# Another table of places for the attention stage's jobs

## The chip, the cores and the metric

The kernel runs on one core of one Trainium2 chip. The metric is the device time of one execution in microseconds (us), as the median of a few runs. TensorE (PE) multiplies matrices, VectorE (DVE) and ScalarE (ACT) read its results from PSUM, GpSimd (POOL) works on SBUF alone, SyncE (SP) issues most transfers. PEld is TensorE's loading of weights, which overlaps its products.

## The reference

Four graph layers work one after the other on 16 graphs of 1024 nodes with 128 features. Only the first of them is touched. It scores pairs of nodes and takes a softmax over the neighbours:

```python
h_self = node_features @ W_self_w + W_self_b
h_nb = node_features @ W_nb_w + W_nb_b
pre = (h_self @ A1_i)[:, :, None, :] + (h_nb @ A1_j)[:, None, :, :] + A1_b
scores = (relu(pre) @ A2_w)[..., 0] + A2_b[0]
scores = where(adjacency == 0, -1e9, scores)
agg = einsum('bij,bjf->bif', softmax(scores), h_nb)
x = layernorm(x + relu(h_self + agg))
```

The adjacency has few edges (a probability of about 0.8% for a pair, and it is symmetric), so the kernel finds the edges and works on them alone. The layers behind (a dilated graph convolution, a dense one and a normalised one) stay as they are.

## The kernel before

`phase_att` does the first layer. The nodes of a graph are cut into NG = 10 groups of W = 104 nodes. A pair of groups (i, j) with j >= i is a *unit*, and a graph has 55. They stand in 5 *blocks* of UNITS = 11: block r holds the pairs of groups r and 9 - r. So there are 16 x 5 = 80 blocks and 880 units. A graph is also called a batch here, and r runs from 0 to 4 within it.

Time is counted in *slots*, one for each unit. Each unit has a gather, a score, a weigh and a scatter. The gather (L554, L559) brings both ends' features for up to 128 edges to a bank `pg`. The score is VectorE's, L571, once for each direction. ScalarE's weigh is an exponential (L581) and a scaled copy (L583) to `hg`. The scatter (L592) adds `hg` into the sums `pa`, with the selection matrix `we`; scatters come some three units behind their gather (BEHIND), and pause at the head of a batch for the units in PAUSE, until the batch before has been collected (L603) and its banks cleared (L300).

The rest of a block's work prepares blocks ahead. Each kind has up to three parts, for units 0 to 3, 4 to 7 and 8 to 10:

- `count` (L401), `offset` (L412) and `rank` (L436, L442) number the edges of a unit; ScalarE copies the results (L408, L417, L449).
- GpSimd's `beyond` (L423) subtracts the offsets from a row of numbers into the tile `g`, of which there is one buffer. VectorE clamps it to 0..1 (`clamp`, L431).
- `step` (L464) turns `g` into selection matrices for an edge's first end; ScalarE copies them (L473) into `oh_b`. `other` (L480) finds the second end; VectorE's comparison (L488) reads it. `widen` (L494) copies both for the gathers.
- `number` (L500, read at L507) and `numbered` (L539, on VectorE) make `we` for the scatters.
- `one_way` (L456) checks on VectorE that the adjacency is symmetric.

For the next batch there are two projections a block (L343, L346; read by ScalarE in L353, L357, L360 and by VectorE in L364 `low` and L367 `add_z`; L371 is `self_score`), and masks: a load of rows, GpSimd's comparison (L316, L318) and a store. For the batch before there is the end: `end_group` (L636, L639 and the statistics L78, L79 on VectorE), a root on GpSimd (`end_root`), `end_norm` (L657 on ScalarE), and transposes (L673, read at L677).

Step, other, rank and its companions, projections and transposes all put their products in the pool `ps_w`, which has **two** PSUM banks. They take turns: a job can start only when all readers of the job two before it are done.

The order is written out. Each job has a place, a number in slots counted from its block's or its batch's first slot:

```python
for key, parts in BANKS:
    ...
        do(at, key, lambda parts: bank_products([(kind, k, block(y)) for kind, k, y in parts]), parts)
        for kind, k, y in parts:
            do(at, READ[kind, k], lambda *key: held.pop(key)(), kind, k, y)
```

All jobs are sorted by place and issued in that order. Each engine keeps its own instructions in it (`as_traced`). A gather stands at u + 0.2, a score at u + 0.55, a scatter at u + 0.8. A place below 0 or above 11 lies in the block before or behind, so that -2.05 is 8.95 of the block before. The places say nothing on time as such: an engine that is done goes on to its next instruction, and one that lacks something holds up all behind it.

Of the kernel before, what the change touches and what calls it, by code (L numbers as in the profile page):

```python
# [130 lines left out]
def as_traced(tc, first):  # L131
# [10 lines left out]


BANKS = (
    (-2.05, (("step", 0),)), (-0.7, (("step", 1),)), (1.5, (("step", 2),)), (2.05, (("other", 0),)),
    (3.1, (("other", 1),)), (4.42, (("rank", 1),)), (5.5, (("rank", 0), ("count", 0),)), (5.58, (("other", 2),)),
    (6.38, (("rank", 2), ("number", 0), ("offset", 0),)),
)
READ = {
    ("step", 0): -1.5, ("step", 1): 0.05, ("step", 2): 1.85, ("rank", 0): 5.82, ("count", 0): 5.75, ("other", 0): 2.5,  # L150
    ("other", 1): 4.36, ("other", 2): 5.9, ("rank", 1): 4.9, ("rank", 2): 7.05, ("offset", 0): 8.31,
    ("number", 0): 7.56,
}
PROJECT = (
    (6.25, 6.42, 6.54, 7.25, 7.33, 6.85, 16.48), (9.85, 9.9, 10.6, 9.95, 11.38, 11.56, 17.53),
)
BEYOND = (3.72, 5.65, 6.42)
CLAMP = (6.38, 8.56, 11.15)
NUMBERED = (1.38, 5.32, 9.9)
ONE_WAY = (-2.25, 5.95)  # L160
WIDEN = (3.38, 6.02, 8.53)
SCORE, WEIGH, SCATTER = 0.55, 1.01, 0.8
COLLECT = (3.51, 3.52, 5.3)
CLEAR = (7.38, 5.9, 6.25)
DIVIDE = 6.45
END_GROUP = (6.58, 9.33, 16.31, 13.9, 28.75, 29.9, 20.38, 27.32, 17.78, 25.5)
END_ROOT = 30.1
END_NORM = (36.72, 38.51, 33.95, 34.54, 38.53, 33.78, 36.32, 43.54, 42.75, 42.53)
END_STORE = 45.1
TURN = ((46.25, 46.65), (47.38, 49.31), (51.45, 51.85))  # L170
MASKS = (-85.1, -82.25, -66.44, -55.48, -52.46, -49.25, -45.47, -42.18, -35.52, -29.18)
AHEAD = {"step": 1, "other": 1, "number": 1, "rank": 2, "count": 3, "offset": 3}
PAUSE = (3, 4, 5, 6)
BEHIND = 3


# [1 line left out]
def phase_att(ctx, tc, t, c, x1_d, x1T_d, mask_d, keep, flags):  # L178
# [207 lines left out]
    def pieces():  # L386
        return [(n0, min(4, UNITS - n0)) for n0 in range(0, UNITS, 4)]

    def block(x):

        if x not in V and x < B * BANDS:
            v = V[x] = Consts()
            v.x = x
            b, v.r = divmod(x, BANDS)
            v.d, v.mt, v.q, v.todo = S[b], MT[b % 2], QS[x % 2], band(v.r)
        return V.get(x)
# [22 lines left out]
    def beyond(v, n0, m):  # L419

        if n0 == 0:
            v.g = sm.tile([P, UNITS, C], F16, name="g", bufs=1)
        nc.gpsimd.tensor_tensor(  # L423
            v.g[:E, n0 : n0 + m, :], k_next[:E].unsqueeze(1).to_broadcast([E, m, C]),
            v.off[:, n0 : n0 + m].unsqueeze(2).to_broadcast([E, m, C]), ALU.subtract,
        )

    def clamp(v, n0, m):

        g = v.g[:E, n0 : n0 + m, :]  # L430
        nc.vector.tensor_scalar(g, g, 1.0, 0.0, op0=ALU.min, op1=ALU.max)  # L431
# [19 lines left out]
    def one_way(v, half):  # L451

        i = (v.r, NG - 1 - v.r)[half]
        at, nb = half * (NG - v.r), NG - i
        junk = sm.tile([P, NG, W], BF16, name="one_way", bufs=1)
        nc.vector.scalar_tensor_tensor(  # L456
            junk[:W, :nb, :], v.q[:W, at : at + nb, :W], EDGE,
            v.mt[:W, i, i * W : NP].rearrange("p (n w) -> p n w", w=W),
            op0=ALU.is_ge, op1=ALU.not_equal, accum_out=seen_one_way[:W, v.x, half : half + 1],
        )  # L460
# [32 lines left out]
    def widen(v, n0, m):  # L493
        nc.scalar.copy(v.ends[:W, n0 : n0 + m], v.o[:W, n0 : n0 + m])  # L494
# [207 lines left out]
    def do(slot, key, f, *args):  # L702
        todo.append((slot + key, len(todo), f, args))

    def scatters(b, n):
        owed.append((b, *divmod(n, UNITS)))
        if not (b and n in PAUSE):
            for _ in range(2 if len(owed) > BEHIND + 1 else 1):
# [34 lines left out]
    for x in range(-3, B * BANDS):  # L743
# [7 lines left out]
        for k in range(3 if x >= 0 else 0):  # L751
            do(at, NUMBERED[k], numbered, b, r, *CHUNKS[k])
        for key, parts in BANKS:
# [5 lines left out]
        for k in range(3):  # L759
            if 0 <= x + 2 < B * BANDS:  # L760
                do(at, BEYOND[k], lambda y, k: beyond(block(y), *pieces()[k]), x + 2, k)
                do(at, CLAMP[k], lambda y, k: clamp(block(y), *pieces()[k]), x + 2, k)
            if 0 <= x + 1 < B * BANDS:
                do(at, WIDEN[k], lambda y, k: widen(block(y), *pieces()[k]), x + 1, k)
        for k in range(2):
            if 0 <= x + 1 < B * BANDS:
                do(at, ONE_WAY[k], lambda y, k: one_way(block(y), k), x + 1, k)
            if 0 <= x and b + 1 < B:
# [4 lines left out]
    for b in range(B - 1):  # L773
# [4 lines left out]
        for s in range(NG):  # L778
            key = MASKS[s] if b else 2 * s - SLOTS + 0.05
            do(at, key - 3 if b else max(key - 3, -SLOTS), load_rows, b + 1, s)  # L780
# [3 lines left out]
        for k in range(3):  # L784
            do(at, COLLECT[k], collect, b, k)
            do(at, CLEAR[k], clear, k)
            do(at, TURN[k][0], open_turn, b, k)
            do(at, TURN[k][1], close_turn, b, k)
        do(at, DIVIDE, end_seen, b)
        do(at, DIVIDE, end_divide, b)  # L790
        do(at, DIVIDE, lambda b: nc.gpsimd.memset(OWN[b % 2][:W, :, 0, F : F + 1], 1.0), b)
        for s in range(NG):
            do(at, END_GROUP[s], end_group, b, ORDER[s])
            do(at, END_NORM[s], end_norm, b, s)
        do(at, END_ROOT, end_root, b)
# [1768 lines left out]
```

## Time and profile before

| | |
|---|---|
| median of 3 runs | 2990.48 us (2989.75 to 2993.03) |
| the profiled execution's own time | 2983.48 us |
| span of its instructions | 2981.2 us |
| mean granted TensorE clock | 0.951 |
| attention stage | to about 1565 us |
| TensorE, VectorE, ScalarE, GpSimd busy, 420 to 720 us | 286.40, 257.49, 251.53, 158.55 us |

A group in the profile has a line of the kernel, an engine, an operation, its tiles (out<-in), shapes, a count, the busy time in us with the mean in ns, and behind the second bar the engine's idle time just before these instructions with what ended it. A timeline row has the start, the duration, the engine, the line and, in brackets, the idle time before it.

### The profile page before, as it was taken

What the parts mean: (1) busy time and instruction counts of PE and PEld (TensorE: products, weight loads), DVE (VectorE), ACT (ScalarE), POOL (GpSimd) and SP (SyncE); (2) the same over time, 40 slices, a digit from 0 to 9 for tenths busy, and PEclk for the clock granted to TensorE, in tenths of its full rate; (3) what the DMA queues carried; (4) which work ended last, traced back from release to release, by engine and by line L of the source; (5) the groups of instructions that cost most, each with busy time, mean ns of one, the idle gap of its engine ahead of it and who ended that gap; (6) DMA issues with size and microseconds to landing.
All of it is one profiled execution on the core that took longest, in us unless ns stands there. A gap on an engine that the chain in (4) does not pass through costs nothing. (4 is left out here: it accounts for less than half of the span.)

```text
span 2981.2 us, 71230 instructions
## 1 busy us (share of the span) xinstructions
PE 2695.8 (90%) x25811; PEld 2407.9 (81%) x25811; DVE 2246.4 (75%) x8654; ACT 1845.1 (62%) x5689; POOL 1261.2 (42%) x1305
## 2 busy tenths in 40 slices
PE   5999999999999999999997888668897999999997
PEld 3888888888888888888897887457786999999996
DVE  5798888988888888988884467756655667777674
ACT  3887888888887888888873233246753433443333
POOL 3655555644555555654223323244433233333321
PEclk8999999999999999999997777789998999999999
DMA  5324332333224332333215442044555254444540
GB/s 160 91 79 114 87 89 68 101 103 84 82 75 115 87 92 73 93 107 88 61 51 168 167 133 79 21 153 170 181 194 212 100 186 177 151 144 181 186 156 17
DMA packets 179962, 348.64 MB, mean 117 GB/s; under 512 B 14148, under 2 KB 89942, under 8 KB 179472
## 3 DMA queue, kind: packets, MB, share of 16 engines
q1 hardware_dynamic: 173584, 328.15, 34.3%
q0 software_dynamic: 4864, 11.63, 1.3%
q10 hardware_dynamic: 1152, 4.19, 0.5%
q8 instruction: 207, 3.39, 0.5%
q14 instruction: 155, 1.27, 0.1%
HBM read 257.87 MB, written 87.03 MB: 116 GB/s over the span
## 5 line engine op out<-in xcount | busy, mean ns | idle before, releaser
L583 ACT ACTIVATE hg<-pg,hg 128x128 f32<-128x128 f32 x1600 | 511.3, 365 | 28.7
L554 PE MATMUL pg<-parts,oh 104*128 104x384 f32 (+1 forms) x1760 | 521.0, 377 | 0.9 <-ACT hg L583 0.8
L316 POOL TENSOR_SCALAR arena<-ld 104x1024 f16<-104x1024 f32 (+1 forms) x150 | 421.7, 2812 | 234.1 <-DMA ld<-in_adjT 234.1
L592 PE MATMUL pa<-hg,we 128*104 128x129 f32 (+1 forms) x3520 | 517.7, 271 | 0.4 <-DVE we L539 0.4
L592 PEld LDWEIGHTS pa<-hg,we 128*104 128x104 f32 x3520 | 465.4, 171 | 10.2 <-DVE we L539 0.8
L571 DVE SCALAR_TENSOR_TENSOR junk<-pg,w_a 128x128 bf16<-128x128 f32 x1600 | 398.4, 283 | 96.9 <-PE pg L559 94.9
L559 PE MATMUL pg<-parts,oh 104*128 104x384 f32 (+1 forms) x1760 | 438.4, 330 | 0.0
L423 POOL TENSOR_TENSOR g<-k_next,off 105x512 f16<-105x512 f16 (+1 forms) x240 | 241.9, 1027 | 315.4 <-PE pw L464 291.7
L559 PEld LDWEIGHTS pg<-parts,oh 104*128 104x128 f32 x1760 | 313.9, 190 | 0.1
L554 PEld LDWEIGHTS pg<-parts,oh 104*128 104x128 f32 x1760 | 276.5, 192 | 27.6 <-issue 15.1
L1667 POOL TENSOR_TENSOR rstd<-ve,mhalf 128x4 f32<-128x4 f32 x96 | 98.1, 1022 | 440.4 <-DVE ve L1666 440.4
L581 ACT ACTIVATE hg<-sc 128x2 f32<-128x2 f32 (+1 forms) x880 | 189.9, 216 | 151.4 <-DVE junk L571 146.7
L1705 ACT COPY xT<-pt 128x512 f32<-128x512 f32 x64 | 37.5, 586 | 374.9 <-PE pt L1704 343.0
L539 DVE TENSOR_TENSOR we<-k_id,ids 128x832 f32<-128x832 f16 (+1 forms) x240 | 254.4, 1060 | 0.0
L494 ACT CAST oh<-oh_b 104x1024 fp32r<-104x1024 bf16 (+1 forms) x240 | 235.2, 980 | 2.4 <-DVE oh_b L488 2.4
L343 PE MATMUL pw<-w_all,xT 128*104 128x512 f32 x320 | 170.2, 613 | 14.2 <-DMA xT<-in_xTp 9.3
L488 DVE TENSOR_TENSOR oh_b<-pw,k_slot_edge 104x512 bf16<-104x512 f32 (+1 forms) x240 | 153.8, 641 | 15.8 <-PE pw L480 15.4
L364 DVE TENSOR_TENSOR parts<-pw,parts 104x384 fp32r<-104x384 f32 x160 | 88.3, 552 | 86.5 <-ACT own L360 85.6
L473 ACT CAST oh_b<-pw 104x512 bf16<-104x512 f32 (+1 forms) x240 | 131.1, 547 | 0.7 <-PE pw L464 0.3
L571 DVE DVE_READ_ACCUMULATOR junk<-pg,w_a 128x1 f32 x1600 | 131.0, 82 | 0.0
L456 DVE SCALAR_TENSOR_TENSOR one_way<-qs,arena 104x1040 bf16<-104x1040 f16 (+9 forms) x160 | 125.7, 786 | 2.2 <-ACT qs L449 2.2
L1508 DVE BATCH_NORM_STATS2 stats<-pt 128x6 f32<-128x512 f32 x120 | 79.0, 691 | 62.6 <-PE pt L1504 61.4
(368 smaller groups left out, 6477.3 us busy)
## 6 DMA issues: line engine op xcount, KB each, us to landing
ld<-in_adjT SPq DMA_DIRECT2D x135, 416.0 KB
keep_adj<-in_adjT SPq DMA_DIRECT2D x8, 4096.0 KB
adj<-in_adjT SPq DMA_DIRECT2D x8, 4096.0 KB
mask_d<-arena SPq DMA_DIRECT2D x144, 208.0 KB
hT_d<-uT SPq DMA_DIRECT2D x48, 512.0 KB
h<-hT_d SPq DMA_DIRECT2D x48, 512.0 KB
arena<-mask_d SPq DMA_DIRECT2D x11, 2048.0 KB
hT<-hT_d SPq DMA_DIRECT2D x32, 512.0 KB
```

Of the source, the lines that this page charges most:

```text
L316: engine.tensor_scalar(mt[:n, s, :N], ld[:n], 0.0, None, op0=ALU.is_gt)
L343: nc.tensor.matmul(pw[:W], d.xT[:, s * W : (s + 1) * W], w_all, start=True, stop=False, skip_group_check=True)
L423: nc.gpsimd.tensor_tensor(v.g[:E, n0 : n0 + m, :], k_next[:E].unsqueeze(1).to_broadcast([E, m, C]), v.off[:, n0 : n0 + m].unsqueeze(2).to_ ...
L488: nc.vector.tensor_tensor(v.o[:W, n0 : n0 + m, 1, :], pw[:W, : m * C].rearrange("p (n c) -> p n c", c=C), k_slot_edge[:W].unsqueeze(1).to_ ...
L494: nc.scalar.copy(v.ends[:W, n0 : n0 + m], v.o[:W, n0 : n0 + m])
L539: nc.vector.tensor_tensor(we[:, :n, :], k_id.unsqueeze(1).to_broadcast([P, n, W]), V[b * BANDS + r].ids[:, 2 * lo : 2 * hi].unsqueeze(2).t ...
L554: nc.tensor.matmul(flat[:, first : 3 * F], own, d.parts[i][:W, p, first:], start=p == 0, stop=False, skip_group_check=True,)
L559: nc.tensor.matmul(pg[:, 1::step, :], other, reversed_parts(d.parts[j][:W, p, :], step), start=False, stop=p == 1, skip_group_check=True,)
L571: nc.vector.scalar_tensor_tensor(junk, pg[:, 1 + e, :], 0.0, w_a2, op0=ALU.max, op1=ALU.mult, accum_out=d.sc[:, at + e : at + e + 1],)
L581: nc.scalar.activation(hg[:, :ways, F], d.sc[:, at : at + ways], AF.Exp)
L583: nc.scalar.activation(hg[:, e, :F], pg[:, 3 - 3 * e, :], AF.Copy, scale=hg[:, e, F : F + 1])
L592: nc.tensor.matmul(PA[bank][:W, at : at + part.stop - part.start], we[:, 2 * (u - lo) + e, :], hg[:, e, part], start=False, stop=True, ski ...
```

## The change

Only the table of places is changed. The functions, the instructions and the sizes stay.

```diff
 BANKS = (
-    (-2.05, (("step", 0),)), (-0.7, (("step", 1),)), (1.5, (("step", 2),)), (2.05, (("other", 0),)),
-    (3.1, (("other", 1),)), (4.42, (("rank", 1),)), (5.5, (("rank", 0), ("count", 0),)), (5.58, (("other", 2),)),
-    (6.38, (("rank", 2), ("number", 0), ("offset", 0),)),
+    (-1.75, (("step", 0),)), (0.85, (("step", 2),)), (1.82, (("other", 0),)), (3.05, (("step", 1),)),
+    (3.31, (("other", 2),)), (4.52, (("rank", 0),)), (5.25, (("other", 1),)), (5.25, (("rank", 1), ("count", 0),)),
+    (6.78, (("rank", 2), ("offset", 0), ("number", 0),)),
 )
 READ = {
-    ("step", 0): -1.5, ("step", 1): 0.05, ("step", 2): 1.85, ("rank", 0): 5.82, ("count", 0): 5.75, ("other", 0): 2.5,
-    ("other", 1): 4.36, ("other", 2): 5.9, ("rank", 1): 4.9, ("rank", 2): 7.05, ("offset", 0): 8.31,
-    ("number", 0): 7.56,
+    ("step", 0): -0.58, ("step", 1): 3.25, ("step", 2): 0.95, ("rank", 0): 4.6, ("count", 0): 5.9,
+    ("other", 0): 2.51, ("other", 1): 5.33, ("other", 2): 3.6, ("rank", 1): 5.82, ("rank", 2): 7.9,
+    ("offset", 0): 7.5, ("number", 0): 6.95,
 }
 PROJECT = (
-    (6.25, 6.42, 6.54, 7.25, 7.33, 6.85, 16.48), (9.85, 9.9, 10.6, 9.95, 11.38, 11.56, 17.53),
+    (6.34, 6.56, 6.78, 6.9, 7.05, 6.85, 16.95), (9.38, 10.15, 11.05, 10.5, 11.5, 11.82, 21.32),
 )
-BEYOND = (3.72, 5.65, 6.42)
-CLAMP = (6.38, 8.56, 11.15)
-NUMBERED = (1.38, 5.32, 9.9)
-ONE_WAY = (-2.25, 5.95)
-WIDEN = (3.38, 6.02, 8.53)
-SCORE, WEIGH, SCATTER = 0.55, 1.01, 0.8
-COLLECT = (3.51, 3.52, 5.3)
-CLEAR = (7.38, 5.9, 6.25)
+BEYOND = (4.78, 5.02, 7.25)
+CLAMP = (5.58, 7.54, 11.36)
+NUMBERED = (0.33, 6.52, 9.53)
+ONE_WAY = (-0.75, 10.32)
+WIDEN = (4.65, 8.75, 7.34)
+SCORE, WEIGH, SCATTER = 0.55, 1.07, 0.8
+COLLECT = (3.52, 5.3, 4.05)
+CLEAR = (5.65, 6.52, 6.15)
 DIVIDE = 6.45
-END_GROUP = (6.58, 9.33, 16.31, 13.9, 28.75, 29.9, 20.38, 27.32, 17.78, 25.5)
+END_GROUP = (6.53, 9.38, 14.54, 15.32, 26.58, 28.65, 18.65, 26.58, 21.95, 29.78)
 END_ROOT = 30.1
-END_NORM = (36.72, 38.51, 33.95, 34.54, 38.53, 33.78, 36.32, 43.54, 42.75, 42.53)
+END_NORM = (33.9, 38.75, 32.45, 33.54, 38.75, 34.75, 39.51, 41.1, 38.95, 36.51)
 END_STORE = 45.1
-TURN = ((46.25, 46.65), (47.38, 49.31), (51.45, 51.85))
-MASKS = (-85.1, -82.25, -66.44, -55.48, -52.46, -49.25, -45.47, -42.18, -35.52, -29.18)
+TURN = ((46.6, 46.78), (48.3, 48.42), (51.65, 52.25))
+MASKS = (-92.44, -86.98, -77.69, -65.52, -59.95, -52.49, -48.64, -45.18, -41.1, -35.67)
-PAUSE = (3, 4, 5, 6)
+PAUSE = (3, 4, 5)
```

BANKS has the places of the bank jobs, READ those of their readers. PROJECT has, for each of the block's two projections, the product, ScalarE's three copies (high, other_z, own), VectorE's `low`, `add_z` and `self_score`. The three numbers of BEYOND, CLAMP, NUMBERED and WIDEN are for the three parts. Bank jobs now alternate more between step and other in the first half of a block, and VectorE's readers stand at other places than the subtractions.

## The prediction

> **What bounds the kernel now.** I read the page's engine line and slices first, then TensorE's groups of instructions in 120 to 1600 us, then the waits of single groups, then the timeline of a few microseconds around a wait.
>
> ```profile
> PE 2695.8 (90%) x25811; PEld 2407.9 (81%) x25811; DVE 2246.4 (75%) x8654; ACT 1845.1 (62%) x5689; POOL 1261.2 (42%) x1305
> PE   5999999999999999999997888668897999999997
> DVE  5798888988888888988884467756655667777674
> ```
>
> The change touches only the attention stage, which is the first 21 slices (to about 1565 us). There TensorE stands at 9 throughout and VectorE at 8 to 9. Busy time by stretch says the same: 120 to 420 us has PE 286.75, DVE 259.03, ACT 252.28 of 300 us. TensorE sets the pace, and its idle part is what another order can win; VectorE is near enough to full to cause it. The groups of instructions of TensorE name the waits:
>
> ```profile
> L464 PE MATMUL pw<-g,k_step 105*128 105x512 f16 (+1 forms) x225 | 82.3, 366 | 20.5 <-DVE z_self L367 18.5 <-ACT hg L581 0.4
> L436 PE MATMUL pw<-cnt,k_offs 104*128 104x416 f16 (+1 forms) x225 | 74.6, 331 | 38.4 <-DVE oh_b L488 38.3
> ```
>
> The last field is idle time just before. A rank job waits 38.3 us in all for the reader of an `other` job, a step job 18.5 us for the last reader of a projection. Over the whole span these are 40.0 and 20.4 us, and the projection's own product waits 4.8 us for L367. All are bank waits: the job wants the PSUM bank used two jobs before, and its reader is late. One case in time:
>
> ```profile
> 480.79 1.04 POOL L423 TENSOR_TENSOR g<-k_next,off 105x512 f16<-105x512 f16 x1
> 480.98 2.73 DVE L539 TENSOR_TENSOR we<-k_id,ids 128x832 f32<-128x832 f16 x1
> 481.80 2.77 POOL L316 TENSOR_SCALAR arena<-ld 104x1024 f16<-104x1024 f32 x1
> 485.53 0.55 DVE L488 TENSOR_TENSOR oh_b<-pw,k_slot_edge 104x384 bf16<-104x384 f32 x1
> 486.13 0.29 PE L436 MATMUL pw<-cnt,k_offs 104*128 104x312 f16 x1 [1.58 <-DVE oh_b L488]
> ```
>
> `numbered` (L539) takes 1.015 us at the median, here 2.73, since it meets a subtraction and then a mask. All behind it on VectorE slips, L488 last, and TensorE stands 1.58 us.
>
> **What the Trainium skill says.** "SBUF — State Buffer", section "Who interferes with whom": a VectorE instruction with two SBUF inputs contends with a GpSimd instruction that reads SBUF, and the later one is blocked for the whole instruction. The trace agrees for subtractions: L636 at 176.35 beside three of them took 1.24 us (median 0.348). It disagrees for masks: L539 above was free again 1.9 us before the 2.77 us mask ended, so only about its first 0.84 us blocks. The same section says that an instruction with one SBUF input does not contend: L488 (PSUM and SBUF) is 545 to 693 ns in two widths, never longer. "PSUM — Partial Sum Buffer", section "Engine vs sequencer instructions": VectorE's and ScalarE's queues are strict first in, first out. The case above shows it.
>
> **The change, part by part.** No instruction is added or removed apart from how they group; each keeps its duration. What changes is who stands before whom.
>
> *Bank order.* Before, per block: step2, other0, other1, rank1, rank0, other2, projection, rank2, step0, projection, step1. After: step2, other0, step1, other2, rank0, other1, rank1, projection, rank2, step0, projection. From the reader's place to the place of the job that wants its bank, the short distances before are 0.43 (projection), 0.48 (rank2 behind other2), 0.68 (other2) and 0.94 slots (step2 behind add_z); after, the shortest are 0.65 (rank1 behind rank0's ScalarE copy) and 0.8 (other2 behind other0). Rank2 then waits for ScalarE's copy of the counts at 5.90, 0.88 slots away with a whole projection between, and step0's projection is 2.2 slots back instead of 1.62. A slot is about 1.7 us (880 in 1495 us). **I credit all three named waits as gone: 40.0 + 18.5 + 4.8 = 63 us.**
>
> *The new wait.* Step2's product moves from 1.5 to 0.85 while clamp2, the VectorE clamp that it reads, moves from 0.15 to 0.36, behind numbered0 (from 1.38 to 0.33). One distance falls from 1.35 to 0.49 slots and the 1 us instruction steps in front. This can be priced from rows of before:
>
> ```profile
> 797.65 0.29 DVE L571 SCALAR_TENSOR_TENSOR junk<-pg,w_a 128x128 bf16<-128x128 f32 x1 [0.64 <-PE pg L559]
> 798.08 0.26 DVE L431 TENSOR_SCALAR g<-g 105x384 f16<-105x384 f16 x1
> 800.27 1.01 DVE L539 TENSOR_TENSOR we<-k_id,ids 128x832 f32<-128x832 f16 x1
> ```
>
> From the start of gather 10's last product (797.28): 0.37 until its score starts (797.65), 0.43 for two scores (to 798.08), 0.93 for numbered0 to make way for the next, 0.26 for clamp2, 0.05 to wake TensorE (L488 ends 805.30, L436 starts 805.35): 2.04 us, or 1.83 where unit 10 has one score (r = 1). TensorE has in between scatter, gather 0, scatter. In five consecutive blocks before, gather 10's last product to the next gather 1 took 1.49, 1.69, 2.07, 2.08, 1.67 us (next r = 4, 0, 1, 2, 3); less 0.20 for step1, which no longer lies there, 1.29 to 1.88. The wait is 0.75, 0.55, 0, 0.16, 0.57 us. Three blocks have more: an end_group (1.13 us: 483.63 to 484.76) now stands at 10.95 in r = 1, between score 10 and numbered0, so r = 2 becomes 1.3; one at 9.38 in r = 0 before numbered2 makes the longer chain (numbered2, both one_way halves, now together at 10.25 and 10.32, score 10) bind, some 0.6 for r = 1; two late ones in r = 2 add 0.2 for r = 3. Sum 3.95 us a batch, 2.0 in the first batch, which has no end groups: **15 x 3.95 + 2.0 = 61 us added.** Behind step2 stand gather 1 and everything on TensorE; ScalarE's step copy and GpSimd's next subtractions wait for it.
>
> *Subtractions and masks.* `g` has one buffer, so subtractions start when the last step job is done. L423's 291.7 us of GpSimd idle, waiting for L464, show it. That job is now step1 at 3.05 instead of step2 at 1.5: they start 2.6 us later. VectorE then has scores and PSUM readers, which they can't slow; but in r = 1 an end_group at 3.54 meets them, worth 0.9 + 0.7 us of VectorE (L636 1.249 against 0.348, L639 1.016 against 0.293 at most), of which behind score 3 and other2's reader I let 0.3 reach TensorE: 5 us in 15 batches. Masks may catch the clamp chain: 0.84 us at most, estimate 0.15 a block over 75 blocks: 11 us, bounded by 0 and 0.84 x 75 = 63. Clamp0 at 5.58 has 2.5 slots after step1, and its subtraction takes 1.04 us.
>
> *At nothing:* moves of widen, self_score and end_norm (ScalarE and VectorE work whose users are more than a slot away; without that cover each costs its 0.2 to 1 us once per batch or block). Masks move 3 to 11 slots earlier, with their loads and stores on SP in the same number; the last stands 7.9 slots before the first counts that need it instead of 1.7, so a late load (194.7 us of GpSimd waiting for `ld` now) is covered better. PAUSE and CLEAR let scatters resume one unit earlier, the last clear then waiting for collect1 at 5.30; once a batch, 0 to 0.5 us either way. Turn places shift within the same gaps.
>
> Sum: -63 + 61 + 5 + 11 = **+14 us** on the profiled execution's 2983.48, of which I take 13 against roundings. That execution is 7 us under the median 2990.48, so 3003.5 is the median forecast.
>
> **The rivals.** A measurement of this kernel tells about 0.2% (6 us) from no change.
>
> *The trade, slower (forecast):* as summed, 2994 to 3030, likeliest 3003.5. Chance 0.38.
>
> *VectorE's relief wins, faster:* the late readers go and with them the slips behind L539, L636 and L431 in slots 5 to 7; the clamp chain is shorter than priced, because numbered0 and the scores are ready early or because the wait only replaces smaller ones. For it: TensorE's named waits are all in blocks with end groups, and one_way leaves that crowd. Against it: score 10 can't start before gather 10, whatever VectorE's state. It decides when the step2 wait is under 0.6 us a block. At 0.4: -63 + 32 + 5 = -26, that is 2964. Chance 0.37.
>
> *The clamp chain piles up, slower by far:* numbered2, one_way twice, score, numbered0 and clamp2 meet a mask in most blocks (0.84 each) and end groups double it. At 1.7 us a block: -63 + 128 + 5 = +70, 3060. Chance 0.13.
>
> *The change doesn't do what it says, same:* L488 was never slowed by subtractions, so placing readers apart is worth nothing, and waits swap evenly: 2985 to 2996. Chance 0.12.
>
> **Numbers.** Faster 0.37, same 0.12, slower 0.38 + 0.13 = 0.51. The range 2945 to 3055 leaves out the deep end of the gain (all 63 us bring 2927) and half of the pile-up, some 0.16 together. The forecast's own range is 2994 to 3030.
>
> **What would show it.** Right: L436's idle for L488 under 10 us; L464 waiting for L431 (absent now) or for VectorE work beside it, 40 to 90 us; L423 starting some 2.6 us later in a block. Wrong: L464's new idle under 35 us (then faster), or over 110 us (then far slower); or idle of L554 for hg or junk, which I price at nothing.

## The result and the profile after

The changed kernel takes **3080.57 us** (median of 6 runs), the kernel before beside it 2991.76: ratio 1.0295, interval 1.028 to 1.031, about 89 us slower. The forecast, 3003.5, had the side and the place right and the size far too small; the range ended at 3055. The profiled execution of the changed kernel took 3077.34 us (span 3075.5), 94 us over that of before.

Three lines of the page, the same three as before:

```profile
PE 2728.0 (89%) x25811; PEld 2441.5 (79%) x25811; DVE 2263.4 (74%) x8654; ACT 1854.7 (60%) x5689; POOL 1264.9 (41%) x1305
PE   5999999999999999999997889659897899999997
DVE  5788888888888878888885465857665677777774
```

TensorE's busy time rose by 32.2 us, although it does the same 25811 products. Its idle time is 3075.5 - 2728.0 = 347.5 against 285.4: 62.1 us more. Counted for the stage's products alone (lines 290 to 690), idle time rises by 62.3 us (87.5 to 149.8) and busy time by 24.9 (1467.3 to 1492.2). The other 7.3 us of busy time lie behind the stage, where nothing was changed and where the kernels shown here differ by up to 17 us. So the loss in the stage has **two parts: about 62 us of waiting and 25 us of slower products.** My prediction had no term for the second. The slices show neither: rounded to tenths, the stage is 9 throughout, as before.

TensorE's groups of instructions in 120 to 1660 us (busy, mean ns, then idle time just before and what ended it):

```profile
L464 PE MATMUL pw<-g,k_step 105*128 105x512 f16 (+1 forms) x228 | 87.1, 382 | 107.6 <-DVE g L431 93.3 <-ACT hg L583 14.3
L436 PE MATMUL pw<-cnt,k_offs 104*128 104x416 f16 (+1 forms) x225 | 73.7, 328 | 0.0
```

L436's wait for L488 is gone, and L464's for L367 as well. The new wait of L464 for the clamp is there, with 107.6 us where 61 were priced.

The timeline at the start of a block r = 4, where VectorE is on time:

```profile
836.49 0.29 DVE L571 SCALAR_TENSOR_TENSOR junk<-pg,w_a 128x128 bf16<-128x128 f32 x1
836.91 1.02 DVE L539 TENSOR_TENSOR we<-k_id,ids 128x832 f32<-128x832 f16 x1
837.85 0.26 DVE L431 TENSOR_SCALAR g<-g 105x384 f16<-105x384 f16 x1
838.25 0.32 PE L464 MATMUL pw<-g,k_step 105*128 105x384 f16 x1 [0.67 <-DVE g L431]
```

This is the chain as I wrote it: two scores, numbered0, clamp2, step2; the wait is 0.67 us (0.75 priced). And at the start of a block r = 2:

```profile
891.91 1.84 DVE L539 TENSOR_TENSOR we<-k_id,ids 128x624 f32<-128x624 f16 x1
893.89 0.90 DVE L456 SCALAR_TENSOR_TENSOR one_way<-qs,arena 104x728 bf16<-104x728 f16 x1
894.94 0.69 DVE L456 SCALAR_TENSOR_TENSOR one_way<-qs,arena 104x312 bf16<-104x312 f16 x1
895.55 0.28 DVE L571 SCALAR_TENSOR_TENSOR junk<-pg,w_a 128x128 bf16<-128x128 f32 x1
895.98 0.34 DVE L636 SCALAR_TENSOR_TENSOR own<-own,rz 104x128 f32<-104x128 f32 x1
897.11 1.01 DVE L539 TENSOR_TENSOR we<-k_id,ids 128x832 f32<-128x832 f16 x1
898.03 0.26 DVE L431 TENSOR_SCALAR g<-g 105x384 f16<-105x384 f16 x1
898.43 0.48 PE L464 MATMUL pw<-g,k_step 105*128 105x384 f16 x1 [3.57 <-DVE g L431]
```

The same chain with an end_group in it (895.98 to 897.11), which I had counted. But gather 10's last product had started at 893.06, and its score starts only at 895.55, 2.49 us later instead of 0.37: VectorE was still at numbered2 and at both one_way halves. The wait is 3.57 us, where I priced 1.3. Masks on GpSimd had stretched three of VectorE's instructions before it: a clamp to 0.83 us (0.28 without one), numbered2 to 1.84 (0.81) and the second one_way half to 0.69 (0.48).

```profile
889.22 0.83 DVE L431 TENSOR_SCALAR g<-g 105x512 f16<-105x512 f16 x1
891.71 0.38 POOL L318 TENSOR_TENSOR arena<-arena,off_diag 88x104 f16<-88x104 f16 x1
892.06 2.77 POOL L316 TENSOR_SCALAR arena<-ld 104x1024 f16<-104x1024 f32 x1
```

The trace has this block with fewer masks as well. In batch 14 two of its four masks are missing, since they would prepare a batch 16, and the others run earlier; VectorE's jobs from that clamp to clamp2 are the same, in the same order:

```profile
1496.63 0.81 DVE L539 TENSOR_TENSOR we<-k_id,ids 128x624 f32<-128x624 f16 x1
1498.61 0.48 DVE L456 SCALAR_TENSOR_TENSOR one_way<-qs,arena 104x312 bf16<-104x312 f16 x1
1501.58 0.25 DVE L431 TENSOR_SCALAR g<-g 105x384 f16<-105x384 f16 x1
1501.98 0.32 PE L464 MATMUL pw<-g,k_step 105*128 105x384 f16 x1 [1.47 <-DVE g L431]
```

Here gather 10's last product starts at 1498.72 and clamp2 2.86 us later. In batches 1 to 13 it is 4.94 to 4.97 us. So the masks make VectorE late in this block. (Batch 15, which lacks projections and other jobs too, waits 2.05 us.)

The clock after such a wait is seen in the busy time by stretch (start:end, length, busy time and count of PE, PEld, DVE, ACT and POOL, granted clock, DMA share, GB/s):

```profile
900.00:903.00 3.00, 3.00 (x15) 2.90 (x14) 1.71 (x9) 0.83 (x3) 0.00 (x0) 0.50 0.00 0
```

For some microseconds after the wait TensorE ran at half clock. Up to the end of the stage the clock record has 129.9 us at half clock, against 59.3 in the kernel before.

### The profile page after: what moved, and what is told of

Same layout as the page of the kernel before. It is cut to its first block, busy times and chain, and to the rows that moved or that the text cites. A ratio compares the mean times of both kernels' runs of the same rounds, so it can differ in the third digit from the quotient of the medians.

```text
span 3075.5 us, 71208 instructions
## 1 busy us (share of the span) xinstructions
PE 2728.0 (89%) x25811; PEld 2441.5 (79%) x25811; DVE 2263.4 (74%) x8654; ACT 1854.7 (60%) x5689; POOL 1264.9 (41%) x1305
## 5 line engine op out<-in xcount | busy, mean ns | idle before, releaser
L554 PE MATMUL pg<-parts,oh 104*128 104x384 f32 (+1 forms) x1760 | 540.7, 389 | 1.5 <-ACT hg L583 1.3
L592 PE MATMUL pa<-hg,we 128*104 128x129 f32 (+1 forms) x3520 | 532.3, 275 | 0.0
L583 ACT ACTIVATE hg<-pg,hg 128x128 f32<-128x128 f32 x1600 | 510.2, 365 | 28.9
L571 DVE SCALAR_TENSOR_TENSOR junk<-pg,w_a 128x128 bf16<-128x128 f32 x1600 | 399.6, 284 | 151.9 <-PE pg L559 145.1
L316 POOL TENSOR_SCALAR arena<-ld 104x1024 f16<-104x1024 f32 (+1 forms) x150 | 418.1, 2787 | 195.4 <-DMA ld<-in_adjT 195.4
L559 PE MATMUL pg<-parts,oh 104*128 104x384 f32 (+1 forms) x1760 | 445.5, 335 | 0.0
L559 PEld LDWEIGHTS pg<-parts,oh 104*128 104x128 f32 x1760 | 321.8, 195 | 0.0
L554 PEld LDWEIGHTS pg<-parts,oh 104*128 104x128 f32 x1760 | 287.7, 197 | 12.9 <-issue 4.4
L581 ACT ACTIVATE hg<-sc 128x2 f32<-128x2 f32 (+1 forms) x880 | 186.8, 212 | 164.1 <-DVE junk L571 159.6
L539 DVE TENSOR_TENSOR we<-k_id,ids 128x832 f32<-128x832 f16 (+1 forms) x240 | 245.6, 1023 | 3.0 <-ACT ids L507 2.9
L488 DVE TENSOR_TENSOR oh_b<-pw,k_slot_edge 104x512 bf16<-104x512 f32 (+1 forms) x240 | 154.2, 642 | 65.2 <-PE pw L480 64.8
L464 PE MATMUL pw<-g,k_step 105*128 105x512 f16 (+1 forms) x240 | 92.6, 386 | 114.0 <-DVE g L431 99.5
L343 PE MATMUL pw<-w_all,xT 128*104 128x512 f32 x320 | 171.2, 616 | 17.4 <-DMA xT<-in_xTp 11.5
L473 ACT CAST oh_b<-pw 104x512 bf16<-104x512 f32 (+1 forms) x240 | 133.3, 555 | 53.8 <-PE pw L464 52.8
L464 PEld LDWEIGHTS <-k_step 105*128 105x128 f16 x240 | 29.9, 124 | 135.3 <-issue 101.5
L571 DVE DVE_READ_ACCUMULATOR junk<-pg,w_a 128x1 f32 x1600 | 131.5, 82 | 0.0
L1508 DVE BATCH_NORM_STATS2 stats<-pt 128x6 f32<-128x512 f32 x120 | 79.0, 691 | 62.5 <-PE pt L1504 61.4
```

Source lines behind the costliest of these rows:

```text
L316: engine.tensor_scalar(mt[:n, s, :N], ld[:n], 0.0, None, op0=ALU.is_gt)
L343: nc.tensor.matmul(pw[:W], d.xT[:, s * W : (s + 1) * W], w_all, start=True, stop=False, skip_group_check=True)
L488: nc.vector.tensor_tensor(v.o[:W, n0 : n0 + m, 1, :], pw[:W, : m * C].rearrange("p (n c) -> p n c", c=C), k_slot_edge[:W].unsqueeze(1).to_ ...
L539: nc.vector.tensor_tensor(we[:, :n, :], k_id.unsqueeze(1).to_broadcast([P, n, W]), V[b * BANDS + r].ids[:, 2 * lo : 2 * hi].unsqueeze(2).t ...
L554: nc.tensor.matmul(flat[:, first : 3 * F], own, d.parts[i][:W, p, first:], start=p == 0, stop=False, skip_group_check=True,)
L559: nc.tensor.matmul(pg[:, 1::step, :], other, reversed_parts(d.parts[j][:W, p, :], step), start=False, stop=p == 1, skip_group_check=True,)
```

## The experiments

Each group of kernels ran on one chip beside the kernel before, whose median there was between 2978.5 and 2993.9 us; so ratios are compared. 0.001 is 3 us. Runs 4, 12 and 14 to 17 are edits of the kernel before, the others of the changed kernel. In the expectations, a wait "in frame r" stands at the start of block r, and clamp2 "in frame r" at the end of block r. "Half-clock windows" are the 3.41 us units of the clock record at 0.5 between 120 and 1480 us; the changed kernel has 24, the kernel before 6.

| kernel | ratio to before (interval) | L464 waits for the clamp, 120 to 1540 us | half-clock windows |
|---|---|---|---|
| changed | 1.0295 (1.028 to 1.031) | 87.7 us | 24 |
| clamp2 early | 0.993 (0.9903 to 0.9957) | none listed | 2 |
| numbered0 back | 1.010 (1.0063 to 1.0137) | 39.5 | 12 |
| end_group away | 1.0191 (1.0163 to 1.0218) | 69.8 | 9 |
| before + the wait | 1.0118 (1.0093 to 1.0143) | 22.3 | 3 |
| step2 back | 1.0093 (1.0069 to 1.0116) | 39.8 | 11 |
| clamp2 early, end_group away | 0.9926 (0.9907 to 0.9945) | none listed | 0 |
| all end_groups back | 1.0235 (1.0212 to 1.0257) | 85.9 | 25 |
| masks, subtractions back | 1.0234 (1.0213 to 1.0254) | 72.0 | 23 |
| one_way back | 1.0274 (1.0238 to 1.0309) | 61.4 | 25 |
| one_way, masks, subtractions, one end_group | 1.0181 (1.0154 to 1.0208) | 32.4 | 22 |
| clamp2 early, end_group away, add_z early | 0.992 (0.9895 to 0.9944) | none listed | 0 |
| before + bank order | 1.020 (1.0175 to 1.0226) | none listed | 4 |

**1. clamp2 ahead of the chain.**

```diff
-CLAMP = (5.58, 7.54, 11.36)
+CLAMP = (5.58, 7.54, 10.2)
```

> The changed kernel with one place altered: clamp2 (VectorE, L431, the clamp that step2 reads) at 10.2 instead of 11.36, ahead of both one_way halves, score 10, the end_group at 10.95 and numbered0. Theory (the chain of VectorE work ahead of clamp2 makes TensorE wait, and the longest of these waits bring the half-clock stretches): TensorE's idle time at L464 for L431 falls from 99.5 us to under 15, TensorE's busy time from 2728 to about 2700, the time from 3080 to 2955 to 2985, below the kernel before, since its bank waits of 63 us stay gone. Rival A (the alternating bank order is at fault, and step2's wait only covers it): the idle time comes back in front of another job of the banks or a gather, over 3040. Rival B (subtractions and masks meet VectorE more often now, and VectorE is what is late): about half comes back, 3010 to 3040.

Measured: 0.993, so 0.7% *faster than the kernel before*. TensorE's groups in the same stretch:

```profile
L480 PE MATMUL pw<-oh_b,qs 104*128 104x128 bf16 x836 | 85.5, 221 | 24.6 <-DVE z_self L367 14.2 <-ACT oh_b L473 8.9
L464 PE MATMUL pw<-g,k_step 105*128 105x512 f16 (+1 forms) x228 | 83.4, 366 | 10.8 <-ACT oh_b L473 10.0
L436 PE MATMUL pw<-cnt,k_offs 104*128 104x416 f16 (+1 forms) x225 | 73.4, 326 | 0.1
```

One number in the table, the place of one 0.26 us instruction a block, carries the whole loss and more. With clamp2 early, the changed bank order is not slow in the changed kernel. But of the 63 us of old waits that are gone, some 41 us are back here as new waits (24.6 at L480, 10.8 at L464, 4.6 at L554, 1.4 at L343; L480, L554 and L343 had 2.6 together before), chiefly behind the readers L367 and L473. TensorE's idle time in the whole span is 270.4 us, only 15 less than before.

**2. numbered0 behind clamp2 again.**

```diff
-NUMBERED = (0.33, 6.52, 9.53)
+NUMBERED = (1.38, 6.52, 9.53)
```

> The changed kernel with numbered0 (L539, 1.01 us) back at 1.38 instead of 0.33, so behind clamp2 again; clamp2 stays at 11.36. Theory: the chain ahead of clamp2 is 0.93 us shorter in every block. Waits of 0.64, 1.3, 3.72, 1.5 and 0.84 us by frame become about 0, 0.4, 2.8, 0.6 and 0: L464's idle time for L431 falls from 99.5 to 40 to 50 us; the long wait in frame 2 is still 2.8 us, so some half-clock stretches stay: 3005 to 3030. Rival A (bank order): no gain, 3060 to 3085, or the wait moves to another bank job. Rival C (the clock slows for a reason other than the wait): idle falls, TensorE's busy time stays at 2728.

Measured: 1.010, as expected; two thirds of the loss hang on this one VectorE instruction being ahead of clamp2. TensorE's waits, 120 to 1540 us (total, times, longest):

```profile
PE pw L464 <- DVE g L431: 39.5, 31, 2.6
PE pw L480 <- DVE z_self L367: 9.0, 14, 0.9
```

The long wait at the start of r = 2 stays, at 2.6 us.

**3. The end_group out of the chain.**

```diff
-END_GROUP = (6.53, 9.38, 14.54, 15.32, 26.58, 28.65, 18.65, 26.58, 21.95, 29.78)
+END_GROUP = (6.53, 9.38, 14.54, 15.32, 26.58, 28.65, 18.65, 26.58, 23.6, 29.78)
```

> The changed kernel with one end_group a batch at 23.6 instead of 21.95 (1.65 slots later, out of the stretch between score 10 and numbered0). Theory: the wait in frame 2, 3.72 us, falls to 0.8 to 1.5: 33 to 44 us less idle time, and the half-clock stretches that followed the long wait go too, TensorE's busy time 2728 to about 2700: 3080 to 3000 to 3020. Rival C (the slower clock has nothing to do with the long wait): the half-clock stretches stay, busy time stays at about 2725, 3035 to 3050. Rival A and B (bank order, or subtractions): little moves, 3060 to 3080.

Measured: 1.0191, a miss in size. The longest wait fell from 3.6 to 2.5 us, by the end_group's own 1.13 us and no more, not to 0.8 to 1.5. VectorE reaches score 10 late with or without it. The half-clock windows fell from 24 to 9 and TensorE's busy time to 2695.1 us, as the theory of the clock had it and against rival C: in the stage, waits shorter by 18 us brought 20 us less of busy time with them.

**4. The kernel before with the new wait alone.**

```diff
-BANKS = (... (1.5, (("step", 2),)), ...)      READ: ("step", 2): 1.85
+BANKS = (... (0.85, (("step", 2),)), ...)     READ: ("step", 2): 0.95
-CLAMP = (6.38, 8.56, 11.15)    NUMBERED = (1.38, 5.32, 9.9)
+CLAMP = (6.38, 8.56, 11.36)    NUMBERED = (0.33, 5.32, 9.9)
```

> The kernel before with only the chain of the new wait: numbered0 at 0.33, clamp2 at 11.36, step2 at 0.85 and its reader at 0.95; bank order, end_groups, one_way, masks as before. Theory: step2 waits for clamp2 in each block, 0.5 to 0.9 us without an end_group at 10.95: 40 to 70 us of idle time at L464 for L431; its wait for L367 (20 us) goes; L436's wait for L488 stays. 3010 to 3045; no more half-clock than before. What is left up to 3080 belongs to the end_group and the clock. Rival A (bank order): the alternation is absent here, so 2985 to 3000.

Measured: 1.0118, 35 us more. TensorE's groups, 120 to 1660 us:

```profile
L464 PE MATMUL pw<-g,k_step 105*128 105x512 f16 (+1 forms) x227 | 82.7, 365 | 76.3 <-ACT oh_b L473 27.6 <-DVE g L431 24.2 <-DVE z_self L367 22.6
L436 PE MATMUL pw<-cnt,k_offs 104*128 104x416 f16 (+1 forms) x225 | 74.6, 332 | 20.6 <-DVE oh_b L488 20.2
```

L464 waits 76.3 us against 20.5 in the kernel before: 56 us more, close to the 61 that I priced. But only 24.2 us of it are put down to the clamp, L367's 22.6 did not go, as I had expected, 27.6 us for ScalarE's L473 are new, and L436 waits 18 us less. So the ratio lies in the expected range, but this run does not measure the priced chain cleanly. In these surroundings clamp2 starts 1.84 to 2.45 us (medians by r) after gather 10's last product; in the changed kernel it starts 1.74, 1.76, 2.46, 2.77 and 4.96 us after it (medians at the end of r = 3, 4, 0, 2, 1, worked out from start times in the trace). The long delay at the end of r = 1 belongs to the changed surroundings.

**5. step2 back.**

```diff
-BANKS: (0.85, (("step", 2),))    READ: ("step", 2): 0.95
+BANKS: (1.5, (("step", 2),))     READ: ("step", 2): 1.85
```

> The changed kernel with step2's product back at 1.5 and its reader at 1.85; numbered0, clamp2 and all else as changed. Theory (only the distance from clamp2 to step2 is wrong, 0.49 slots): 0.65 slots, some 1.1 us, come back in each block; L464's idle time for L431 falls from 99.5 to 35 to 55 us (frame 2 keeps some 2.5 us), ratio to the kernel before 1.003 to 1.015. Rival A (the alternation of the bank order): 1.02 to 1.03.

Measured: 1.0093, as expected; the longest wait is 1.8 us, where some 2.5 were expected. Distance at either end does the same: moving clamp2's predecessor away (run 2) or step2 (this run) each leaves some 40 us of the wait.

**6. Both edits that gave time.** `CLAMP` as in run 1, `END_GROUP` as in run 3.

> The changed kernel with clamp2 at 10.2 and the one end_group at 23.6, so the two edits that gave time, together. Theory: with clamp2 early (ratio 0.993) what is left is VectorE late at the end of frames 1 and 2, where `other` waits 0.8 to 1.9 us for z_self; the end_group's 1.13 us leaves that place, so this wait falls from 14 to under 6 us and a few more half-clock windows go: ratio 0.984 to 0.991. Rival: once clamp2 is ahead, the end_group is behind nothing that TensorE needs: 0.991 to 0.996.

Measured: 0.9926, the rival's value: the interval takes in run 1's 0.993. With clamp2 ahead, the end_group stands in nobody's way.

**7, 8, 9. What makes VectorE late?** `END_GROUP` as before; `MASKS` and `BEYOND` as before; `ONE_WAY` as before.

```diff
-END_GROUP = (6.53, 9.38, 14.54, 15.32, 26.58, 28.65, 18.65, 26.58, 21.95, 29.78)
+END_GROUP = (6.58, 9.33, 16.31, 13.9, 28.75, 29.9, 20.38, 27.32, 17.78, 25.5)
...
-BEYOND = (4.78, 5.02, 7.25)
+BEYOND = (3.72, 5.65, 6.42)
...
-ONE_WAY = (-0.75, 10.32)
+ONE_WAY = (-2.25, 5.95)
```

> The changed kernel with all ten end_group places as in the kernel before (none then stands between score 10 and numbered0, none beside the subtractions at 3.5 to 4.3 of frame 1 but one). Theory (end_groups feed VectorE's lateness, 8.2 us a batch against 4 without): waits of 0.6 to 1.0 us in every frame, 50 to 65 us of L464 for L431, no long wait and hardly a half-clock window: ratio 1.005 to 1.015. Rival B (masks and subtractions carry the lateness): frame 2 still waits over 2 us, ratio 1.02 to 1.03.

> The changed kernel with masks and subtractions (MASKS, BEYOND) at their places in the kernel before. Theory: the subtractions wait for step1 anyway and a mask costs VectorE at most 0.84 us in ten blocks of 55, so little moves: L464's wait stays 80 to 105 us, ratio 1.022 to 1.032. Rival B (these places make VectorE late): the long wait of frame 2 falls below 2 us, ratio 1.005 to 1.018.

> The changed kernel with both one_way halves (L456) back at 8.75 and 5.95; all else as changed. Second theory (the chain itself was priced right, clamp2 starts 1.74 to 1.76 us after gather 10's last product where VectorE is on time; where it is late, numbered2 and both one_way halves queued between scores 9 and 10 make it late): clamp2 starts 3.3 to 3.7 us after gather 10 instead of 4.97 in frame 1, about 2.0 instead of 2.77 in frame 2, 1.75 to 2.1 instead of 2.41 in frame 0, and stays at 1.75 in frames 3 and 4; L464's wait for L431 60 to 70 us instead of 99.5; ratio to the kernel before 1.012 to 1.020. Rival (VectorE has too much to do in frames 0 to 2 wherever its pieces stand, as the run with the end_groups back suggests): the wait stays over 85 us, ratio 1.022 to 1.032.

Measured: 1.0235, 1.0234 and 1.0274; the last can't be told from the changed kernel's 1.0295. My theory of the end_groups fell in run 7. The waits of TensorE there:

```profile
PE pw L464 <- DVE g L431: 85.9, 69, 2.6
PE pg L554 <- ACT hg L583: 4.7, 16, 0.4
```

The total wait is nearly as long, now shared out over more blocks: clamp2 starts 3.1, 3.8 and 1.9 us after gather 10 at the end of r = 0, 1, 2 (medians; at r = 1 it varies from 2.5 to 4.5). Run 8 took some 18 us off: its ratio lies in the theory's range, its wait, 72.0 us with a longest of 2.3, between the two. The gain is at one place: clamp2 at the end of r = 1 comes after 3.41 us instead of 4.96, and the waits at the start of r = 2 fall from 52.6 to 30.4 us in all, while those of the other blocks rise by 4. So masks and subtractions are the main part of that one wait, though not of the whole loss. Run 9 brought clamp2 at the end of r = 1 from 4.96 to 3.46 us, as expected, but not at the end of r = 0 and 2 (2.4 and 2.9 us), and almost nothing in time: 24.2 us of L464 waiting for ScalarE's L473 came in instead.

**10. Three of them together.** `ONE_WAY`, `MASKS`, `BEYOND` as before, `END_GROUP` as in run 3.

> The changed kernel with one_way, masks and subtractions back at their places and the one end_group at 23.6; numbered0, clamp2, step2 and the bank order stay as changed. Second theory: what makes VectorE late adds up, so with the three feeders gone only the chain that was priced is left, 0.6 to 1.0 us in each block: L464's wait for L431 45 to 60 us, longest under 1.8 us, hardly a half-clock window, ratio 1.003 to 1.012. Rival (VectorE's load as such): over 70 us, longest over 2.3 us, ratio above 1.015.

Measured: 1.0181, a miss for both. The wait for the clamp is down to 32.4 us with a longest of 1.8, better than the second theory said, but the step jobs now wait 23.3 us for ScalarE's L473 and 13.0 us for L581, and half-clock windows stay at 22. In this run other readers come late; why these do was not tested.

**11. add_z earlier.** `CLAMP` and `END_GROUP` as in run 6, and in PROJECT's second row 11.82 becomes 11.56.

> The changed kernel with clamp2 at 10.2, the end_group at 23.6, and the last add_z of the second projection (L367) at 11.56 as in the kernel before, instead of 11.82. Theory: other0's wait for z_self (11.9 us in the run with the first two edits) was a bank wait on this reader and falls under 4 us, ratio 0.986 to 0.991. Rival: the reader is late because VectorE is, not because of its place: ratio as there, 0.991 to 0.995.

Measured: 0.992, as run 6, and L480's wait for z_self stays at 11.6 us: the rival, the reader is late because VectorE is. This is a version below both kernels; it can't be told from runs 1 and 6, which need fewer edits.

**12. The bank order alone.** `BANKS` and `READ` of the changed kernel in the kernel before, clamp2 at 10.2.

> The kernel before with the changed bank order alone (BANKS and READ as changed), and clamp2 at 10.2 so that step2 finds it done; projections, masks, subtractions, one_way, numbered and end_groups as before. Theory (the alternation does what it says): the waits of L436 for L488 (40 us) and of L464 for L367 (20 us) are gone, and some of it comes back as waits of L480: ratio 0.985 to 0.997. Rival A (the alternation is at fault): 1.005 or more.

Measured: 1.020, a plain miss. L436 still waits 30.7 us for L488 and 14.4 for ScalarE's L449, and gathers wait 19.6 us for hg. The order that alternates is no gain by itself. In the changed kernel the 63 us went with other moves beside it (projections and VectorE's jobs stand at their old places here); which of them it takes, no run shows. TensorE's busy time in the stage rose by 21 us here although half-clock windows fell to 4: its products are no longer than before (3495 us summed one by one, 3492 before), but overlap less. In the changed kernel and in run 16 the products themselves are longer (3549 and 3520 us).

**13. numbered0 back where clamp2 is early.** As run 6, with `NUMBERED` of run 2.

> The changed kernel with clamp2 at 10.2, the end_group at 23.6 and numbered0 back at 1.38. Theory: with numbered0 (1.01 us) out of the way of the last add_z (L367 at 11.82), other0's wait for z_self (12 us) and its half-clock windows go: ratio 0.985 to 0.991. Rival: what other0 waits for is set elsewhere: 0.991 to 0.996.

Measured: 1.004 (1.0027 to 1.0053), a miss on the far side. L480 waits 16.2 us for L583, which was not there, and z_self's wait stays at 11.3. So numbered0 at 0.33 is *worth* 0.0114 (34 us) once clamp2 stands ahead of it, and costs 0.0195 (58 us) with clamp2 behind it.

**14 to 17. A wait of known size in the kernel before.** The clamp gives the same values however often it is done, so it can hold up VectorE, and with it step2, at will:

```diff
     def clamp(v, n0, m):
         g = v.g[:E, n0 : n0 + m, :]
-        nc.vector.tensor_scalar(g, g, 1.0, 0.0, op0=ALU.min, op1=ALU.max)
+        for _ in range(26 if n0 and m < 4 and v.x % 5 in (0,) else 1):
+            nc.vector.tensor_scalar(g, g, 1.0, 0.0, op0=ALU.min, op1=ALU.max)
```

The other three have 15 times in (0, 1, 4), then 16 times in (0,) and 8 times in (0, 1, 4). Lines below the edit carry numbers one higher.

> The kernel before with clamp2 of one block in five (step2 at the start of frame 4) done 26 times over instead of once; the clamp gives the same values each time. Estimate 0.2 us each, 5.2 us more on VectorE, of which some 1.8 us lie inside the distance to step2: one wait of about 3.4 us a batch, 50 to 60 us in all. Theory of the clock (a window of 3.41 us in which TensorE stood about half or more is followed by one at half clock): one or two half-clock windows a batch, TensorE's busy time 2696 to 2720 to 2735, ratio to the kernel before 1.024 to 1.034. Rival C (the slower clock of the changed kernel had nothing to do with its long wait): busy time within 5 us of 2696, ratio 1.015 to 1.021.

> The kernel before with clamp2 of three blocks in five (step2 at the start of frames 3, 4 and 0) done 15 times over: some 3 us more each, so three waits of about 1.2 us a batch, about the same total of 50 to 60 us. Theory of the clock: no window stands half empty, half-clock windows stay as few as in the kernel before, busy time 2690 to 2705, ratio 1.015 to 1.022 although VectorE has 1.7 times as much to repeat. Rival C: the same ratio as with one long wait.

> As the run with one long wait, with 16 clamps instead of 26: 15 more at the 0.26 us measured there, 3.9 us, less the 0.5 us of slack measured there: one wait of about 3.4 us a batch, 45 to 52 us in all. Theory of the clock: a half-clock stretch of 3.4 or 6.8 us after nearly every such wait, TensorE's busy time 2715 to 2730, so 1.2 to 2.4 us more a batch than the wait itself; ratio to the kernel before 1.022 to 1.030. Rival C: busy time stays at 2696, ratio 1.014 to 1.019.

> As the run with three waits, with 8 clamps instead of 15: 7 more at 0.26 to 0.30 us, 1.8 to 2.1 us, less a slack of 0.5 to 0.8 us: three waits of 1.0 to 1.5 us a batch, 45 to 65 us in all. Theory of the clock: these fill under half of a window, few half-clock windows beyond those of the kernel before, busy time 2690 to 2705, ratio 1.014 to 1.022. Rival C: the extra busy time is that of VectorE's load or of the total wait, so as much as with one long wait or more: 2715 to 2735.

| kernel | ratio (interval) | step2's wait for the clamp | TensorE busy | half-clock windows |
|---|---|---|---|---|
| one, 26 clamps | 1.0369 (1.0352 to 1.0387) | 84.6 us in 14 | 2723.6 | 28 |
| three, 15 clamps | 1.0723 (1.0705 to 1.0741) | 127.9 in 39 | 2793.0 | 63 |
| one, 16 clamps | 1.0201 (1.0176 to 1.0226) | 46.5 in 15 | 2723.5 | 18 |
| three, 8 clamps | 1.0217 (1.0193 to 1.0241) | 41.4 in 30 | 2731.7 | 23 |

The first two doses came out too large (6.0 and 3.3 us a wait, for 3.4 and 1.2 expected: the slack of step2 is some 0.5 us and not 1.8, and a repeated clamp took 0.26 to 0.30 us). The third has the wait as planned, 3.1 us a batch, and a ratio just under the theory's range (1.0201 for 1.022 to 1.030) and over the rival's. Its waits, 120 to 1540 us, and its busy time by stretch around one wait:

```profile
PE pw L465 <- DVE g L432: 46.5, 15, 3.1
```

```profile
733.40:736.80 3.40, 0.29 (x2) 0.16 (x2) 3.05 (x12) 1.00 (x3) 0.00 (x0) 0.99 0.71 184
736.80:740.20 3.40, 3.40 (x17) 3.22 (x17) 3.40 (x11) 1.56 (x6) 3.03 (x3) 0.51 0.09 33
740.20:743.60 3.40, 3.40 (x32) 3.04 (x31) 1.81 (x12) 3.11 (x9) 0.58 (x1) 1.00 0.16 63
```

The first stretch has TensorE almost empty (0.29 us busy), at full clock. The next, at 0.51, finishes 17 products, the one after that, at 1.00, 32. Busy time rose by 27.7 us to 2723.5, as the theory of the clock had it (2715 to 2730) and not the rival (2696); 20.5 us of this lie in the stage, from one wait of 3.1 us a batch. That shows the second part of the loss by itself. The fourth run did not come out short and even: its busy time, 2731.7, lies where the rival put it, but its 30 waits have a longest of 2.7 us, with other waits beside them, so it has half-clock windows as well and does not tell long waits from short ones.

What does tell is a count over the 19 kernels shown here, cut into the clock record's units of 3.41 us: of 7309 windows (120 to 1480 us) whose predecessor had TensorE idle for under 0.45 of its length, 63 were at half clock, 51 of them behind one that was at half clock itself; of 77 with 0.45 to 0.5, 52; of 187 with more than 0.5, all 187.

## Why the prediction was wrong in size

**The bound** was read rightly: TensorE sets the time of this stage, its idle part is what the order moves, and VectorE's lateness makes it.

**The credit of 63 us.** The named waits did go (L436 for L488: 38.4 to 0.0). But where the new wait is out of the way, in runs 1, 6 and 11, TensorE's idle time is only 15 us under that of before and the kernel 21 to 24 us faster: other readers are late in the banks' new order. In the changed kernel 6.1 us at L480 show openly; that step2's wait covers the rest of this was not tested. My sum had no term for what comes next after a wait is taken away.

**The chain of step2** was found and, where VectorE is on time, priced to within 0.03 us: clamp2 comes 1.74 and 1.76 us after gather 10's last product at the end of r = 3 and 4, where my 0.37 + 0.43 + 0.93 gives 1.73. **The step that failed is the sum of 3.95 us a batch**, in the three blocks with end groups. I took VectorE to begin score 10 0.37 us after the product in all blocks but one, and allowed the masks 0.15 us a block. Measured from the trace (start to start, less the shortest such interval), step2 waits 0.64, 1.1 to 1.5, 3.72, 1.3 to 1.8 and 0.84 us at the start of r = 0 to 4, some 8 us a batch; priced were 0.55, 0.6, 1.3, 0.75 and 0.75. The end_group in the chain was sized right (1.13 us; run 3 gives 1.1). What lacked was the lateness that VectorE brings along. Step2's idle time is 113.8 us over the span (99.5 put down to the clamp and 14.3 to L583), where 61 were priced: 53 us too few. Half of that is the 2.1 us at the end of r = 1, in 13 batches some 27 us, and the masks make it: in batch 14, without two of them, clamp2 comes after 2.86 us, which is the priced 1.73 + 1.13, and the wait is 1.47 us for 1.3 priced. Most of the rest is at the start of r = 1 and 3 (42.0 us for 21 priced). Runs 7 to 10 show no single piece that carries it: with the end_groups back the lateness lands in other blocks, with masks and subtractions back these two waits rise by 4 us, and one_way back takes 0.002 off the ratio, within the noise. What this rest is shared out to stays open.

**Subtractions and masks (5 + 11 us).** A block's first subtraction starts 5.98 us after gather 0's last product instead of 2.64 (medians): 3.3 us later, 2.6 predicted. Reading the stage's stretched VectorE instructions off the trace, those over 0.1 us longer than the shortest of their kind and shape, gives 107.6 us against 98.5: 9 us more on VectorE, and no relief. The rival "VectorE's relief wins" had nothing to stand on. The clamps' part of it doubled, from 18.9 to 39.8 us. The total was near what I took; where it fell was not: my 11 us for the masks are too few beside the 27 at the end of r = 1, where three instructions were stretched in one block.

**The clock** was no term at all, and cost about a quarter: 24.9 us of busy time in the stage. The Trainium skill has the rule of which I made no use: "TensorE: Matmul & The Clock Gate", Part 1, says that TensorE falls to half clock after an idle window of about 3.4 us and that these windows run freely. The window is confirmed here (3.41 us in the clock record); the condition is harder than the page has it, since a window idle by just over half was enough in every case counted. A wait of 3.57 us, or a shorter one of which over half a window (1.7 us) falls into one, is therefore paid more than once.

**The rivals.** The one that comes nearest is "the clamp chain piles up": its 1.7 us a block is near what was measured (8 us in five blocks), and its 3060 lacks the clock's 25 us and has the whole credit of 63. Its cause, masks in most blocks, is right for one block in five, the end of r = 1; run 8 leaves 1.0234 of 1.0295. Of my own signs, "over 110 us at L464, then far slower" was met in the whole span (99.5 us for the clamp and 14.3 for L583), and L554's idle for hg stayed at 1.3 us, as said.

## What to carry to other kernels

When a reader moves towards its writer, don't price the chain from the block where every engine is on time: take, for each kind of block, how late the writer's engine already comes to the chain's first instruction, and which of GpSimd's jobs stretch the instructions before it: the queue passes all of that on. Moving the one small instruction that TensorE waits for ahead of the long ones in VectorE's queue was worth 0.036 of the time here. And when TensorE is the bound, look at what each wait does to its clock in the stretch behind it, as the busy time by stretch shows it.

## What the runs showed of the hardware

- Half clock after a half-idle window: 187 of 187 windows behind one idle for more than 0.5 of 3.41 us, 63 of 7309 behind one idle for less than 0.45, and 51 of these 63 behind one at half clock. In run 16 one wait of 3.1 us a batch added 20.5 us of busy time in the stage over 15 waits, some 1.4 us each.
- A mask (L316, 2.77 us) beside a two-input VectorE instruction blocks it only at first: L539 of the changed kernel met one at 892.06 and was done at 893.75, 1.08 us before the mask's end at 894.83.
- The clamp (L431) has one SBUF input and is slowed beside GpSimd all the same. In the 15 kernels that do it once, 1845 clamps had no GpSimd instruction beside them, and none took over 0.30 us; of the 1755 that had one, 899 took over 0.4 us, up to 1.24. VectorE's readers of PSUM were not slowed: L571 never took over 0.294 us and L488 never over 0.693, before or after the change.
